# Graph attention and a gated FFN on one core: attention in slots of two units, with steps of the output projection in the last slots

## The chip, the cores and the metric

The kernel runs on one core of a Trainium2 chip. The metric is the device time of one execution in microseconds (us). All times below are in us unless a unit stands beside them. Lower is better.

## The reference

The input `x` has 384 rows (nodes) of 1024. A layer of graph attention with 16 heads of 64 is followed by a gated FFN, both with a residual.

```python
def _L0_gnn_ref(x, edge_index, edge_type, edge_type_weights, wq, bq, ...):
    q = x @ wq.T + bq
    k = x @ wk.T + bk
    v = x @ wv.T + bv
    q2 = (q @ wiq.T + biq).reshape(N, H, D).transpose(1, 0, 2)
    k2 = (k @ wik.T + bik).reshape(N, H, D).transpose(1, 0, 2)
    v2 = (v @ wiv.T + biv).reshape(N, H, D).transpose(1, 0, 2)
    mask = _build_mask(edge_index, edge_type, edge_type_weights, x.dtype)
    scores = jnp.einsum('hnd,hmd->hnm', q2, k2) * scale + mask[None]
    attn = jax.nn.softmax(scores, axis=-1)
    out = jnp.einsum('hnm,hmd->hnd', attn, v2)
    out = out.transpose(1, 0, 2).reshape(N, OUT_F)
    return out @ wo.T + bo

def _L0_ffn_ref(x, w1_w, w1_s, w2_w, w2_s, h1_w, h1_s, h2_w, h2_s, w3_w, w3_s):
    h = jax.nn.silu(_tlin(x, w1_w, w1_s)) * _tlin(x, w2_w, w2_s)
    h = jax.nn.gelu(_tlin(h, h1_w, h1_s), approximate=False)
    h = jax.nn.gelu(_tlin(h, h2_w, h2_s), approximate=False)
    return _tlin(h, w3_w, w3_s)

x = x + _L0_gnn_ref(_layernorm(x, axis=-1), edge_index, ...)
x = x + _L0_ffn_ref(_layernorm(x, axis=-1)[None], ...)[0]
```

The mask is built from 12288 edges: minus infinity where there is no edge, and a positive weight by the type of the edge where there is one.

## The kernel before

All matrices of attention are float32. The kernel works through these stages, and TensorE (PE) goes through them in this order:

- The layer norm of `x` and its transposition into `xT`, behind 34 transposes of the identity that nobody reads (`warm`, L222).
- Four projections with `matmul_T` (L138): q, q2, v and later k. Each output chunk of 128 columns is a sum of 8 matmuls of 384 columns in one bank of the PSUM pool `ps_mm`, and ScalarE (ACT) moves it out with its bias. v2 is made with `matmul_R` (L147), whose matmuls have 512 columns. Meanwhile GpSimd (POOL) scatters the 12288 edges into a table in DRAM, from which the mask `nmask` is read back.
- Attention. A *unit* `u` is one tile of 128 query rows for one pair of heads: 8 pairs times 3 row tiles make 24 units. `scores(u)` is two matmuls of 64 rows, one per head. `exponentials(u)` is, per head, one reduce on VectorE (DVE), which adds the mask, writes `s` and finds the row's minimum `lo` (the scores are negated), and one exp on ACT, which writes `e` and the row's sum. `normalised(u)` is a reciprocal and two multiplications of `e` on DVE. `transposed(u)` is 6 transposes on PE into two banks `pp`; ACT copies the first to `pT`, DVE the second. When the three units of a pair are done, `weighted(pair)` makes `av` in 6 matmuls, two heads side by side in the array's columns, and ACT copies it to `aT`.
- k2, the projection of k, is not made ahead as a whole. `project_k2` (L421) is a generator of 64 steps, one matmul each. Chunks 0 to 2 (24 steps) come first, and the remaining 40 steps are spread over the loop of units.
- The output projection with `wo`: 6 groups of 8 matmuls of 512 columns, one for each row tile `t` and half (`project_out`, L536). Behind each group DVE adds the residual (L539) and takes statistics (L113), and behind each second group comes the layer norm of the tile.
- The FFN (`rest`, L581). It has two forms. The fast one multiplies in a rounded type, with the activations split into two rounded parts. It is exact if the weights of the FFN have no low mantissa bits. To know that, the kernel reads all FFN weights as integers in 16 pieces (`inspect`, L176): per piece one DMA `raw` and two operations on DVE that OR the bits together into `bits` (L182). `gather_bits` (L548) reduces `bits` to one word per partition, the matmul `fl` (L575) adds the words over the partitions, and the result is the flag of the branch (L566, L684). 6 of the 16 pieces are read during the projection of k. The other 10 are read around wo: 5 ahead of it, 3 after its first group, and 2 after the first row tile's layer norm.

The kernel writes the order of SP, ACT, DVE and PE out by hand: each engine works in the order in which the program names its instructions (`manual_schedule`, L58). The order inside the loop of attention before the change is, for each unit `u`:

```python
scs = scores(u) if u < units else None
pt = transposed(u - 2) if 2 <= u < units + 2 else None
if pt:
    nc.scalar.copy(*pt[0])
if 1 <= u <= units:
    normalised(u - 1)
if scs:
    exponentials(u, scs)
if pt:
    nc.vector.tensor_copy(*pt[1])
if u >= 3 and (u - 3) % NT == NT - 1:
    weighted((u - 3) // NT)
```

Then comes the unit's share of k2, two steps in most units. The last steps of k2 are done in unit 19. [...]

## Time and profile before

| What | Value |
|---|---|
| Runs | 426.0, 426.37, 426.67 (median 426.37) |
| Profiled execution, its own time | 426.34 |
| Its span, first to last instruction | 424.6 |
| PE busy | 408.7 (96%) |
| DVE, ACT, POOL busy | 177.4, 100.0, 109.5 |
| Matmuls of k2 (L426) | 128 records, 45.5 busy |
| Matmuls of scores (L442), av (L484) | 96 records each |
| Matmuls of wo (L152) | 96 records, 41.8 busy |
| Mean granted clock of TensorE | 0.994 |

A float32 matmul appears as two records of the profile, so 128 records of k2 are 64 matmuls; a transpose is one record. Matmuls are pipelined, so the busy time of a record overlaps that of the next, and the time between two starts says more than a record's length. The chain of waits is followed back from the last instruction: at each step to what released it, or to the instruction ahead of it on its engine. Its times and the times of the timeline count from the start of the span.

### The profile page before, as it was taken

The page shows a single profiled execution, that of the slowest core. Times are in us where ns is not written, and L with a number is a line of the kernel's source. Part 1 is how long each engine was busy: PE and PEld are TensorE (multiplying, and loading weights), DVE is VectorE, ACT ScalarE, POOL GpSimd, SP SyncE. Part 2 cuts the span into 40 slices and gives each one's busy share as a digit, 9 for nine tenths or more (in the row PEclk, how much of TensorE's full clock was granted, in tenths as well). Part 3 has the DMA queues.
Part 4 walks back from the last instruction along what each step waited for, and adds up shares of the span by engine and source line. Part 5 has one row for each costly group of instructions (what it writes and reads, how often), then busy time and mean ns, then how long its engine had stood idle before and what let it go on. Part 6 is the DMA issues. An engine that isn't in the chain of part 4 may idle for free.

```text
span 424.6 us, 4305 instructions
## 1 busy us (share of the span) xinstructions
PE 408.7 (96%) x1549; PEld 242.4 (57%) x1549; DVE 177.4 (42%) x563; ACT 100.0 (24%) x220; POOL 109.5 (26%) x117
## 2 busy tenths in 40 slices
PE   7899999999999999999999999999999999999991
PEld 6555555555555444455555454455544445799971
DVE  5646879300000010124000476666678755232462
ACT  4511111111111000011111565455462002222510
POOL 3023335234747475734473000000000000200000
PEclk9999999999999999999999999999999999999997
DMA  7699855986050505085425060000196100920012
GB/s 266 215 357 260 267 164 189 393 313 199 0 199 0 199 6 192 19 319 177 180 55 200 2 175 25 0 0 2 34 377 243 42 0 2 298 99 0 2 72 80
DMA packets 29207, 59.64 MB, mean 140 GB/s; under 512 B 4384, under 2 KB 7296, under 8 KB 29056
## 3 DMA queue, kind: packets, MB, share of 16 engines
q1 hardware_dynamic: 22016, 49.89, 34.0%
q0 software_dynamic: 6880, 9.03, 7.4%
q10 hardware_dynamic: 288, 0.41, 0.3%
q8 instruction: 14, 0.23, 0.2%
q14 instruction: 9, 0.07, 0.0%
HBM read 57.06 MB, written 2.26 MB: 140 GB/s over the span
## 4 chain that ended last, share of the span: by engine, by line
PE 90%; DMA 3%; DVE 3%; ACT 2%; issue 0%; SPq 0%; ACTq 0%; DVEq 0%
PE ps L143 39%; PE ps L152 19%; PE ps L426 9%; PE ps L590 6%; PE sc L442 5%; PE pp L475 4%; PE av L484 4%; PE ps L603 3%; DMA out<-y 2%; DMA xs<-in_x 1%; PE pt L531 1%; ACT e L459 1%; DVE y L680 1%; DVE y L681 1%; DVE st L113 0%
## 5 line engine op out<-in xcount | busy, mean ns | idle before, releaser
L353 POOL DMA_INDIRECT tab<-val,cell x96 | 94.1, 980 | 119.2 <-DMA tab<-val,cell 65.1
L426 PE MATMUL ps<-kT,wik 128*128 128x384 f32 x128 | 45.5, 492 | 0.0
L337 DVE SCALAR_TENSOR_TENSOR jk<-kr,key,later 128x256 bf16<-128x256 f32 x96 | 40.0, 479 | 13.0 <-DMA kr<-keyd 12.6
L402 DVE TENSOR_TENSOR v<-ps,row 128x512 f32<-128x512 f32 x6 | 4.2, 692 | 96.1 <-PE ps L152 96.1
L456 DVE CUSTOM_DVE_ANT_0 s<-sc,nmask 128x384 f32<-128x384 f32 x48 | 24.7, 552 | 43.5 <-PE sc L442 43.5
L152 PE MATMUL ps<-wo,aT 128*128 128x512 f32 x96 | 41.8, 593 | 0.0
L143 PE MATMUL ps<-xT,wq 128*128 128x384 f32 x128 | 41.5, 487 | 0.3 <-ACT xT L257 0.3
L143 PE MATMUL ps<-qT,wiq 128*128 128x384 f32 x128 | 41.4, 486 | 0.0
L143 PE MATMUL ps<-xT,wv 128*128 128x384 f32 x128 | 41.4, 486 | 0.0
L143 PE MATMUL ps<-xT,wk 128*128 128x384 f32 x128 | 41.4, 486 | 0.0
L152 PE MATMUL ps<-wiv,vT 128*128 128x512 f32 x96 | 41.4, 592 | 0.0
L143 PEld LDWEIGHTS ps<-xT,wk 128*128 128x128 f32 x128 | 24.3, 190 | 17.2 <-issue 0.5
L143 PEld LDWEIGHTS ps<-xT,wq 128*128 128x128 f32 x128 | 24.2, 190 | 17.2 <-ACT xT L257 0.5
L143 PEld LDWEIGHTS ps<-qT,wiq 128*128 128x128 f32 x128 | 24.3, 190 | 17.0
L143 PEld LDWEIGHTS ps<-xT,wv 128*128 128x128 f32 x128 | 24.3, 190 | 17.0
L426 PEld LDWEIGHTS ps<-kT,wik 128*128 128x128 f32 x128 | 22.7, 190 | 15.7 <-issue 4.1
L152 PEld LDWEIGHTS ps<-wiv,vT 128*128 128x128 f32 x96 | 18.2, 190 | 22.7 <-issue 22.5
L152 PEld LDWEIGHTS ps<-wo,aT 128*128 128x128 f32 x96 | 18.0, 190 | 22.1 <-issue 21.3
L459 ACT ACTIVATE e<-s,lo 128x384 f32<-128x384 f32 x48 | 29.1, 608 | 4.6 <-DVE lo L456 4.5
L182 DVE TENSOR_TENSOR bits<-bits,raw 128x512 int32<-128x512 int32 x32 | 22.1, 691 | 15.7 <-DMA raw<-in_w 14.8
L590 PE MATMUL ps<-x,w 128*128 128x384 f32 (+2 forms) x176 | 25.8, 306 | 0.0
L590 PEld LDWEIGHTS ps<-x,w 128*128 128x128 f32 x176 | 25.1, 190 | 0.5 <-issue 0.5
(110 smaller groups left out, 360.7 us busy)
## 6 DMA issues: line engine op xcount, KB each, us to landing
kr<-keyd SPq DMA_DIRECT2D x11, 576.0 KB, 5.8
raw<-in_w SPq DMA_DIRECT2D x12, 512.0 KB, 4.2
w<-in_w POOLq DMA_DIRECT2D x3, 2048.0 KB, 9.3
wiq<-in_wiq SPq DMA_DIRECT2D x2, 2048.0 KB, 12.8
wv<-in_wv SPq DMA_DIRECT2D x2, 2048.0 KB, 15.3
wiv<-in_wiv SPq DMA_DIRECT2D x2, 2048.0 KB, 14.4
wk<-in_wk SPq DMA_DIRECT2D x2, 2048.0 KB, 8.3
wik<-in_wik SPq DMA_DIRECT2D x2, 2048.0 KB, 7.7
```

Source lines behind the costliest of these rows:

```text
L143: nc.tensor.matmul(ps[:, :N], lhsT=w[:, k, o * P:(o + 1) * P], rhs=src[:, k, :], start=(k == 0), stop=(k == nk - 1))
L152: nc.tensor.matmul(ps[:, :w.shape[2]], lhsT=src[:, k, t * P:(t + 1) * P], rhs=w[:, k, :], start=(k == 0), stop=(k == nk - 1))
L182: nc.vector.tensor_tensor(bits, bits, raw[:, h * FH:(h + 1) * FH].bitcast(I32), op=ALU.bitwise_or)
L337: nc.vector.scalar_tensor_tensor(jk[:, :w], krf[:, j * P:j * P + w], key[:, c:c + 1], later[:, :w], op0=ALU.is_equal, op1=ALU.mult, accum_ ...
L353: i = nc.gpsimd.indirect_dma_start(out=tab, in_=val[:, c:c + 1], in_offset=None, out_offset=bass.IndirectOffsetOnAxis(ap=cell[:, c:c + 1], ...
L426: nc.tensor.matmul(ps[:, :N], lhsT=wik[o // 4][:, k, o % 4 * P:(o % 4 + 1) * P], rhs=kT[:, k, :], start=(k == 0), stop=(k == KF - 1))
L442: nc.tensor.matmul(sc[:, :N], lhsT=q2T[r, pair, t * P:(t + 1) * P], rhs=k2T[r, pair, :], start=True, stop=True)
L456: nc.vector.tensor_tensor_reduce(s, sc[:, :N], nmask[:, t, :], 1.0, 3e38, op0=ALU.add, op1=ALU.min, accum_out=lo)
L459: nc.scalar.activation(e, s, AF.Exp, bias=lo, scale=-1.0, accum_out=dens[u][:, j:j + 1])
L475: nc.tensor.transpose(pt[:, m, :], e[:, m * P:(m + 1) * P], ident)
L484: nc.tensor.matmul(av[j * D:(j + 1) * D, :N], lhsT=v2[:, m, h * D:(h + 1) * D], rhs=pTs[pair % 2][:, j * NT + m, :], start=(m == 0), stop= ...
L590: nc.tensor.matmul(ps[:, rows], lhsT=w[:, k, o * P:(o + 1) * P], rhs=x[:, k, rows], start=n == 0, stop=n == len(todo) - 1)
```

## The change

- Attention goes in 13 slots: unit 0, eleven slots of two units, unit 23. A slot is: the scores of its units, the reduces and exps of its units, the av of a pair that is complete since two slots ago, the transposes of the first unit of the slot before, the slot's share of k2, and the transposes of the second one. A unit is normalised in its own slot.
- The share of k2 is 7 steps in slot 0, and 3 or 4 in slots 1 to 10. In slots 11 and 12 three steps each of the first group of wo take its place. After the last slot stand more steps of wo: one and six, then the transposes of unit 23, one and four, the last av, and three. So three groups of wo are at 7 of 8 steps when the loop ends; `project_out` finishes them first.
- Two pieces of the inspection come ahead of the last transposes; the rest stay at their places.
- The exp writes over the buffer that the reduce wrote: one pool `e` of 9 buffers in place of `s` (3) and `e` (6).
- A first exp of one column (`loaded`) stands ahead of k2, and with it the load of the exp table on ACT.
- PSUM: `ps_mm` has 2 banks instead of 3; `ps_ff`, now opened ahead of attention with 4, holds the scores and wo's groups; `ps_pt` has 2. Behind attention the transposes of `x2` have their own 2 banks (`ps_out`), and the FFN's banks go two of `ps_ff`, one of `ps_mm`.

```diff
-    ps_mm = ctx.enter_context(tc.tile_pool(name="ps_mm", bufs=3, space=bass.MemoryType.PSUM))
+    ps_mm = ctx.enter_context(tc.tile_pool(name="ps_mm", bufs=2, space=bass.MemoryType.PSUM))
...
+    wos = [queue.pop(0)[0] for _ in range(2)]
     aT = act.tile([P, KF, N], FP, tag="xT", name="aT")
+    ps_ff = ctx.enter_context(tc.tile_pool(name="ps_ff", bufs=4, space=bass.MemoryType.PSUM))
+
+    def bank(name="ps"):
+        return ps_ff.tile([P, 512], FP, tag="ff", name=name)
+
+    def out_steps(ps, t, half, k0, k1):
+
+        for k in range(k0, k1):
+            nc.tensor.matmul(ps, lhsT=aT[:, k, t * P:(t + 1) * P], rhs=wos[half][:, k, :],
+                             start=k == 0, stop=k == KF - 1)
+        return k1
...
-                s = ap.tile([P, N], FP, tag="s", name="s", bufs=3)
+                e = ap.tile([P, N], FP, tag="e", name="e", bufs=9)
                 lo = small.tile([P, 1], FP, name="lo")
-                nc.vector.tensor_tensor_reduce(s, sc[:, :N], nmask[:, t, :], 1.0, 3e38,
+                nc.vector.tensor_tensor_reduce(e, sc[:, :N], nmask[:, t, :], 1.0, 3e38,
                                                op0=ALU.add, op1=ALU.min, accum_out=lo)
-                e = ap.tile([P, N], FP, tag="e", name="e", bufs=6)
-                nc.scalar.activation(e, s, AF.Exp, bias=lo, scale=-1.0,
+                nc.scalar.activation(e, e, AF.Exp, bias=lo, scale=-1.0,
                                      accum_out=dens[u][:, j:j + 1])
...
         units = H // 2 * NT
+        slots = [[0], *([u, u + 1] for u in range(1, units - 1, 2)), [units - 1]]
+        loaded = small.tile([P, 1], FP, name="loaded")
+        nc.scalar.activation(loaded, eps, AF.Exp)
         k2 = project_k2()
-        done, rest_k2 = 0, (KF - AHEAD) * KF
+        done, pairs, left = 0, 0, (KF - AHEAD) * KF
         for _ in range(AHEAD * KF):
             next(k2)
-        for u in range(units + 3):
...
+        begun = []
+        for s, new in enumerate(slots):
+            old = slots[s - 1] if s else []
+            scs = [scores(u) for u in new]
+            for u, sc in zip(new, scs):
+                exponentials(u, sc)
+            if s >= 2 and max(slots[s - 2]) >= NT * pairs + NT - 1:
+                weighted(pairs)
+                pairs += 1
+            for i in range(2):
+                if i < len(old):
+                    pt = transposed(old[i])
+                    nc.scalar.copy(*pt[0])
+                    nc.vector.tensor_copy(*pt[1])
+                if i < len(new):
+                    normalised(new[i])
+                if i == 0:
+                    share = min(7 + -(-(left - 7) * s // (len(slots) - 3)), left) - done
+                    for _ in range(share):
+                        next(k2)
+                    done += share
+                    if s >= len(slots) - 2:
+                        if not begun:
+                            begun.append((bank(), 0))
+                        ps, k = begun.pop()
+                        begun.append((ps, out_steps(ps, 0, 0, k, k + 3)))
+        inspect_more(False, 2)
+        out_steps(begun[0][0], 0, 0, KF - 2, KF - 1)
+        begun = [(begun[0][0], KF - 1), (bank(), KF - 1)]
+        out_steps(begun[1][0], 0, 1, 0, KF - 2)
+        pt = transposed(units - 1)
+        nc.scalar.copy(*pt[0])
+        nc.vector.tensor_copy(*pt[1])
+        out_steps(begun[1][0], 0, 1, KF - 2, KF - 1)
+        begun.append((bank(), 4))
+        out_steps(begun[2][0], 1, 0, 0, 4)
+        weighted(pairs)
+        out_steps(begun[2][0], 1, 0, 4, KF - 1)
+        begun[2] = (begun[2][0], KF - 1)
...
-    ps_ff = ctx.enter_context(tc.tile_pool(name="ps_ff", bufs=5, space=bass.MemoryType.PSUM))
+    ps_out = ctx.enter_context(tc.tile_pool(name="ps_out", bufs=2, space=bass.MemoryType.PSUM))
...
     def project_out(t, half, st):
         c = slice(half * FH, (half + 1) * FH)
-        ps = matmul_R(wos[half], aT, t)
+        ps, k = begun.pop(0) if begun else (bank(), 0)
+        out_steps(ps, t, half, k, KF)
         nc.vector.tensor_add(xs[:, t, c], ps, xs[:, t, c])
         statistics(t, st, half)
...
-    inspect_more(True, 2)
+    inspect_more(True)
     for t in range(NT):
         st = small.tile([P, 2, 6], FP, name="st")
         project_out(t, 0, st)
...
         def bank():
+            taken.append(len(taken) % 3)
+            if taken[-1] == 2:
+                return ps_mm.tile([P, 512], FP, tag="mm", name="ps")
             return ps_ff.tile([P, 512], FP, tag="ff", name="ps")
```

The loop over the row tiles behind `inspect_more(True)` is as before. For `t` = 0 it is: first half of `project_out`, three pieces of the inspection, second half, layer norm, the last two pieces, `gather_bits`. For `t` = 1: both halves, layer norm, `fl`, the flag, the transposes of the first tile. For `t` = 2: first half, the load of the flag, the transposes of the second tile, second half, layer norm.

## The prediction

> **What bounds the kernel now.** I read the shares of the span first, then the chain of waits, then the timeline of the stretch that is changed.

> ```profile
> PE 408.7 (96%) x1549; PEld 242.4 (57%) x1549; DVE 177.4 (42%) x563; ACT 100.0 (24%) x220; POOL 109.5 (26%) x117
> PE 90%; DMA 3%; DVE 3%; ACT 2%; issue 0%; SPq 0%; ACTq 0%; DVEq 0%
> ```

> TensorE is busy for 96% of the span and is 90% of the chain, so only two things help: less time for the same matmuls, or fewer waits of PE. The chain inside attention, in order of time (start, length, what), shows the period:

> ```profile
> 250.06 0.84 PE sc L442 x4
> 250.90 0.81 PE pp L475 x6
> 251.71 2.09 PE av L484 x12
> 253.79 1.49 PE ps L426 x4
> 255.28 0.85 PE sc L442 x4
> 256.13 0.80 PE pp L475 x6
> 256.93 1.29 PE ps L426 x4
> ```

> A step of k2 or of scores is two records. Two steps of k2 take 1.29, so one takes 0.645. The scores of a unit are two heads on two halves of the array's rows: their streams overlap, yet the group takes 0.845, 0.20 more than one stream. The share of k2 that follows an av takes 1.49, again 0.20 more. The timeline shows PE's waits (in brackets, with what ended them):

> ```profile
> 240.68 1.39 PE L442 MATMUL sc<-k2T,q2T 64*128 64x384 f32 x4 [0.96 <-DVE lo L456]
> 313.89 1.39 PE L442 MATMUL sc<-k2T,q2T 64*128 64x384 f32 x4 [0.86 <-DVE lo L456]
> ```

> Attention on the chain runs from 235.06 (first scores) to 322.57 (first step of wo): 87.5. Its regular pieces are 24 x 0.845 scores, 24 x 0.805 transposes, 40 x 0.645 for k2, 8 x 2.09 for av and 6 x 0.20 after av: 20.3 + 19.3 + 25.8 + 16.7 + 1.2 = 83.3. So 4.2 are waits, nearly all at the two ends, where k2 has not yet spread or has run out.

> Behind attention I read VectorE, because wo and the inspection of the weights' bits share that stretch:

> ```profile
> 320.28 7.22 DVE L182 TENSOR_TENSOR bits<-bits,raw 128x512 int32<-128x512 int32 x10
> 329.74 0.69 DVE L539 TENSOR_TENSOR xs<-ps,xs 128x512 f32<-128x512 f32 x1 [2.24 <-PE ps L152]
> 331.07 4.30 DVE L182 TENSOR_TENSOR bits<-bits,raw 128x512 int32<-128x512 int32 x6
> 336.53 0.69 DVE L539 TENSOR_TENSOR xs<-ps,xs 128x512 f32<-128x512 f32 x1 [1.16 <-PE ps L152]
> 339.29 2.86 DVE L182 TENSOR_TENSOR bits<-bits,raw 128x512 int32<-128x512 int32 x4
> 342.18 2.23 DVE L553 TENSOR_TENSOR bits<-bits 128x256 int32<-128x256 int32 x9
> 344.71 0.69 DVE L539 TENSOR_TENSOR xs<-ps,xs 128x512 f32<-128x512 f32 x1
> 350.16 0.19 PE L575 MATMUL fl<-ones,bitf 128*1 128x1 f32 x2
> ```

> The matmul `fl` needs `bitf`, which VectorE finishes just before 344.71. PE comes to `fl` at 350.16, 5.4 later. That is the slack the change spends.

> **The change, part by part.** All against the profiled execution: 426.34, of which 424.6 is span; the median of the runs is 426.37, 0.03 off.

> *Slots of two units.* The two scores groups stand back to back, so I take 2 x 0.645 + 0.20 = 1.49 for four heads instead of 1.69: 11 slots save 2.2. Two groups in a row do not occur in the trace. The bounds are nothing saved (each group pays its 0.20) and 2.2; I take 2.2, because the 0.20 appears where the kind of matmul changes, not inside a run of one kind. An av now comes after scores and before transposes; the 0.20 of k2 after an av goes (1.2). Transposes after an av stand in the trace at 318.10 and show no such surplus: their first copy starts 0.58 after them, as elsewhere. Av straight after scores is unseen: bounds 0 and 7 x 0.20 = 1.4 lost; I take 0, since av after transposes shows none.

> *Waits inside attention.* I laid the new order of PE, VectorE and ScalarE out by these durations: a reduce each 0.48, an exp each 0.61, a copy 0.48, a normalisation 0.87. Unit 0's softmax took 5.1 (235.06 to 240.16), of which 1.28 was the table load that is moved ahead; the 3.8 left lie under seven steps of k2 (4.5), so the wait at 240.68 goes. The wo steps cover the last slots and the last transposes. What is late next is slot 10, with three steps of k2 and no av. The last transposes of the slot could start at 1.49 + 0.8 + 1.94 + 0.4 = 4.6 after its start. The copy that frees their bank stands behind four exps on ScalarE: first reduce 1.55 after the start (VectorE still normalises the slot before), 0.65 to the first exp, 4 x 0.61, copy 0.48: 5.1. So 0.5, and with 0.2 elsewhere 0.7. The same laying-out gives 3.6 of the 4.2 that the kernel before shows, so I book 1.2. PSUM costs nothing: a projection's bank has 5.2 until its next use and the eviction takes 0.58; were that cover gone, each of 40 chunks would cost 0.6.

> *wo moved forward.* 18 of the 48 steps of 0.858 (two records of 0.429) now lie before the last av. They are the same work: 15.4. The end of the last av becomes 235.06 + 2 x 0.845 + 11 x 1.49 + 19.3 + 25.8 + 16.7 + 15.4 + 1.2 = 331.6. Before, the comparable point is 322.57 + 15.4 = 338.0. The gain up to here is 6.4.

> *The price behind it.* Wo's first three groups are finished almost together, so from the last av PE has only 3 + 3 + 8 = 14 steps, 12.0, before it reaches `fl`. VectorE's queue in front of `bitf` is: two pieces of bits early and three more under the last wo steps (hidden), then the first add, which needs 4 steps and a latency of 0.3 (3.75 after the av); add and statistics, 1.33 (329.74 to 331.07); six bit operations, 4.30; second add, statistics, moments and normalisation, 2.76 (336.53 to 339.29); four bit operations, the tree and the casts, 5.42 (339.29 to 344.71). The sum is 17.6. PE waits 17.6 - 12.0 = 5.6 at `fl`, with everything queued behind it: the transposes of x2, the last 16 steps of wo, the flag, the FFN. The loads of raw are not late: the last trio needs the first pT buffer free, over 20 before VectorE reads it. Net 6.4 - 5.6 = 0.8 gained, 425.5, if nothing else happens.

> *The clock.* An idle PE of 5.6 occurs nowhere inside the kernel before. Only its two ends show what idleness does. The table by stretches (length, PE busy, PEld, DVE, ACT, POOL, then granted clock):

> ```profile
> 418.00:419.00 1.00, 0.00 (x0) 0.00 (x0) 0.00 (x0) 0.00 (x0) 0.00 (x0) 1.00 0.32 111
> 419.00:420.00 1.00, 0.00 (x0) 0.00 (x0) 0.00 (x0) 0.00 (x0) 0.00 (x0) 0.75 0.10 30
> 420.00:421.00 1.00, 0.00 (x0) 0.00 (x0) 0.43 (x1) 0.00 (x0) 0.00 (x0) 0.50 0.02 7
> ```

> The last matmul ends at 415.25; the granted clock is halved from about 419.5, 4.25 later. At the other end, the loads of the warming transposes (min/median/max ns, first and last start):

> ```profile
> L225 PEld LDWEIGHTS pw<-ident x6: 231/231/231, 4.3 to 5.4; 128*128 128x128 f32 x6
> L225 PEld LDWEIGHTS pw<-ident x10: 139/140/142, 8.2 to 9.2; 128*128 128x128 f32 x10
> ```

> They begin at 2.33 and turn from 231 to 140 ns at about 6.4, after 4.0 of work; the clock column reads 1.00 there, so only durations show it. 5.6 exceeds 4.25, so I expect half the clock when `fl` starts, for about 4.0, which loses half of that: 2.0. Bounds: 0 (the clock holds) and 4.0 (twice as long a slow stretch). I take 2.0.

> [...]

> *The FFN.* Same matmuls, six banks in turn and two for transposes instead of five; its waits on the chain (1.7 at 397, 1.7 at 403) are on gelu, not on banks: 0.

> Sum: 426.34 - 6.4 + 5.6 + 2.0 = 427.5.

> **The rivals.**
> 1. *The clock holds.* [...] For it: 5.6 is only 1.3 over the one drop that the trace shows. Against: the drop is there. Time 425.5, on the faster side.
> 2. *Attention gains less.* Each scores group pays its 0.20 (2.2) and av after scores too (1.4): 427.5 + 3.6 = 431.1. For it: 0.845 against 0.645 in every unit. Against: no surplus where transposes meet av.
> 3. *VectorE is not late at `fl`* (the queue is shorter than I read): no wait, no clock: 426.34 - 6.4 = 419.9. Against: every operation of it is in the rows above, in that order.

> **How the numbers follow.** A measurement of this kernel can tell about 0.2% (0.85) from no change. The forecast (wait and clock) has 0.61, with its own range 426.3 to 429.5; rival 1 has 0.24, between 424.5 and 426.5; rival 2 has 0.09; rival 3 has 0.02; 0.04 is left for more gain in attention, near 424. Slower: about three quarters of the forecast (0.46), all of rival 2: 0.55. Within 0.2%: 0.15 of the forecast, 0.11 of rival 1: 0.26. Faster: the rest, 0.19. For the range I take 425.0 to 430.0: it holds the forecast, most of rival 1, and leaves out rivals 2 and 3.

> **What would show it.** Right: scores x8 of about 1.5 in one slot; no wait of PE near 240; an idle PE of 5 to 6 ended by `bitf` in front of `fl`; a clock of 0.5 in the stretch behind it, and steps of wo of twice 0.858 there. Wrong: `fl` without a wait, a clock of 1.00 throughout, or waits of PE on VectorE in every slot.

## The result, and the profile after

The changed kernel takes 425.25 us (median of 12 runs, 423.69 to 427.02) against 426.37; the ratio is 0.9975 with a 95% interval of 0.9958 to 0.9991. The median is lower by a quarter of a per cent. The forecast was 427.5, on the other side. The median stands in a gap: six of the 12 runs lie between 423.69 and 424.79, six between 425.70 and 427.02; the experiments e6 and e8 come back to these two levels.

The profiled execution took 424.21, of which the span is 422.4. The shares of the span and of the chain of waits:

```profile
PE 404.6 (96%) x1549; PEld 245.0 (58%) x1549; DVE 176.0 (42%) x563; ACT 98.1 (23%) x221; POOL 110.9 (26%) x117
PE 90%; DVE 5%; ACT 2%; DMA 2%; issue 1%; SPq 0%; ACTq 0%; DVEq 0%
```

VectorE, 3% of the chain before, is now 5%. The chain inside attention (start, length, what), a slot without an av and one with:

```profile
257.48 1.49 PE sc L460 x8
258.97 0.80 PE pp L492 x6
259.77 2.58 PE ps L444 x8
262.36 0.65 PE pp L492 x6
263.01 1.49 PE sc L460 x8
264.50 2.09 PE av L501 x12
266.59 0.80 PE pp L492 x6
267.39 1.94 PE ps L444 x6
```

The scores of two units take 1.49, as forecast, and av straight behind scores still takes 2.09. The transposes are 0.80 behind scores or av, but only 0.65 behind k2. The timeline of PE shows a single wait above 0.5 inside attention, and then the one behind it:

```profile
301.85 0.55 PE L492 MATMUL pp<-ident,e 128*128 128x128 f32 x3 [0.67 <-ACT pTb L530]
329.96 12.28 PE L423 MATMUL ps<-wo,aT 128*128 128x512 f32 x28
347.64 0.19 PE L611 MATMUL fl<-ones,bitf 128*1 128x1 f32 x2 [5.39 <-DVE bitf L592]
347.76 1.97 PE L572 MATMUL pt<-ident,xn 128*128 128x128 f32 x8
349.52 8.38 PE L423 MATMUL ps<-wo,aT 128*128 128x512 f32 x16
```

The wait at 240.68 is gone, the one in slot 10 is there (0.67), and `fl` waits 5.39 for `bitf`. VectorE works through it:

```profile
342.08 2.86 DVE L182 TENSOR_TENSOR bits<-bits,raw 128x512 int32<-128x512 int32 x4
...
347.43 0.15 DVE L592 CAST bitf<-bits 128x1 f32<-128x1 int32 x1
```

The table by stretches (length, PE, PEld, DVE, ACT and POOL busy, granted clock) shows the clock halved during the wait and for a while behind it:

```profile
345.00:346.00 1.00, 0.00 (x0) 0.00 (x0) 0.92 (x3) 0.00 (x0) 0.00 (x0) 0.70 0.00 0
346.00:347.00 1.00, 0.00 (x0) 0.00 (x0) 0.84 (x5) 0.00 (x0) 0.00 (x0) 0.50 0.00 0
352.00:353.00 1.00, 1.00 (x3) 0.45 (x2) 0.38 (x1) 1.00 (x3) 0.00 (x0) 0.89 0.00 0
```

Up to the FFN the two profiles differ by little: its first matmul starts at 365.42 before and at 365.07 after. The other 1.9 of the spans' 2.2 lies at the end, 1.7 of it in one write of the output, whose lines the change does not touch. This is the last write on the chain of the kernel before:

```profile
416.41 4.05 DMA out<-y
```

And this is the one on the chain of the changed kernel:

```profile
415.96 2.39 DMA out<-y
```

### The profile page after: what moved, and what is told of

It reads as the page before. It is cut to its first block, busy times and chain, and to the rows that moved or that the text cites. A ratio compares the mean times of both kernels' runs of the same rounds, so it can differ in the third digit from the quotient of the medians.

```text
span 422.4 us, 4320 instructions
## 1 busy us (share of the span) xinstructions
PE 404.6 (96%) x1549; PEld 245.0 (58%) x1549; DVE 176.0 (42%) x563; ACT 98.1 (23%) x221; POOL 110.9 (26%) x117
## 4 chain that ended last, share of the span: by engine, by line
PE 90%; DVE 5%; ACT 2%; DMA 2%; issue 1%; SPq 0%; ACTq 0%; DVEq 0%
PE ps L143 39%; PE ps L152 10%; PE ps L444 9%; PE ps L423 8%; PE ps L626 6%; PE ps L639 5%; PE av L501 4%; PE pp L492 4%; PE sc L460 4%; DVE bits L182 2%; DMA xs<-in_x 1%; PE pt L572 1%; DVE st L113 1%; ACT e L476 1%; DMA out<-y 1%
## 5 line engine op out<-in xcount | busy, mean ns | idle before, releaser
L353 POOL DMA_INDIRECT tab<-val,cell x96 | 95.4, 993 | 118.1 <-DMA tab<-val,cell 67.5
L423 PE MATMUL ps<-wo,aT 128*128 128x512 f32 x96 | 43.8, 609 | 0.0
L444 PE MATMUL ps<-kT,wik 128*128 128x384 f32 x128 | 43.5, 488 | 0.0
L152 PE MATMUL ps<-wiv,vT 128*128 128x512 f32 x96 | 41.4, 592 | 0.0
L474 DVE CUSTOM_DVE_ANT_0 e<-sc,nmask 128x384 f32<-128x384 f32 x48 | 23.9, 553 | 37.8 <-PE sc L460 37.8
L476 ACT ACTIVATE e<-e,lo 128x384 f32<-128x384 f32 x48 | 29.0, 604 | 25.1 <-DVE lo L474 25.1
L152 PEld LDWEIGHTS ps<-wiv,vT 128*128 128x128 f32 x96 | 18.2, 190 | 22.7 <-issue 22.5
L182 DVE TENSOR_TENSOR bits<-bits,raw 128x512 int32<-128x512 int32 x32 | 22.1, 691 | 14.4 <-DMA raw<-in_w 13.6
L626 PE MATMUL ps<-x,w 128*128 128x384 f32 (+2 forms) x176 | 25.8, 307 | 0.0
```

The lines of the kernel that those rows point to most:

```text
L152: nc.tensor.matmul(ps[:, :w.shape[2]], lhsT=src[:, k, t * P:(t + 1) * P], rhs=w[:, k, :], start=(k == 0), stop=(k == nk - 1))
L182: nc.vector.tensor_tensor(bits, bits, raw[:, h * FH:(h + 1) * FH].bitcast(I32), op=ALU.bitwise_or)
L353: i = nc.gpsimd.indirect_dma_start(out=tab, in_=val[:, c:c + 1], in_offset=None, out_offset=bass.IndirectOffsetOnAxis(ap=cell[:, c:c + 1], ...
L423: nc.tensor.matmul(ps, lhsT=aT[:, k, t * P:(t + 1) * P], rhs=wos[half][:, k, :], start=k == 0, stop=k == KF - 1)
L444: nc.tensor.matmul(ps[:, :N], lhsT=wik[o // 4][:, k, o % 4 * P:(o % 4 + 1) * P], rhs=kT[:, k, :], start=(k == 0), stop=(k == KF - 1))
L474: nc.vector.tensor_tensor_reduce(e, sc[:, :N], nmask[:, t, :], 1.0, 3e38, op0=ALU.add, op1=ALU.min, accum_out=lo)
```

## The experiments

Ten kernels ran. Each expectation names a theory and a rival, and what each of them would show. Ratios are against the kernel before, measured beside them, with 95% intervals.

**The flag late (e1).** The last two pieces and the tree stand behind the second tile's layer norm, and `make_flag` (the lines of `fl` and the flag's copy) in the middle of wo's last group:

```diff
         elif t == 2:
-            low_bits = nc.values_load(flag[0:1, 0:1], min_val=0, max_val=P * 0xFFF)
             transpose_x2(1)
+            ps = bank()
+            out_steps(ps, t, 1, 0, 4)
+            flag = make_flag()
+            out_steps(ps, t, 1, 4, 7)
+            low_bits = nc.values_load(flag[0:1, 0:1], min_val=0, max_val=P * 0xFFF)
+            begun.append((ps, 7))
         project_out(t, 1, st)
         layernorm(t, xn[:, t, :], st)
-        if t == 0:
-            inspect_more(False, len(pieces))
-            bitf = gather_bits()
-        elif t == 1:
...
+        if t == 1:
+            transpose_x2(0)
+            inspect_more(False, len(pieces))
+            bitf = gather_bits()
```

> The changed kernel with the tail of the inspection reordered: the last two pieces and the reduction of the bits come behind the second tile's layer norm on VectorE, and the matmul fl stands in the middle of the last group of wo. Nothing is left out. Theory (what attention saved goes to PE's wait at fl and to the slow clock behind it): fl waits for nothing, the granted clock stays 1.00 from 330 to 400, and the time falls by the wait of 5.4 and the 2.3 that the slow stretch cost (transposes of x2 1.90 instead of 0.87, 16 records of wo 8.17 instead of 6.87): 425.3 - 7.7 = 417.6. Rival (VectorE bounds this stretch, so the wait only moves to the transposes of x2 or to the flag): 423 or more, with a PE wait of 3 or more somewhere between 340 and 370.

Measured: 418.45, ratio 0.9816 (0.9791 to 0.984). PE's timeline and one row of the table by stretches:

```profile
342.15 1.06 PE L572 MATMUL pt<-ident,xn 128*128 128x128 f32 x8
...
354.32 0.19 PE L597 MATMUL fl<-ones,bitf 128*1 128x1 f32 x2
```

```profile
345.00:350.00 5.00, 5.00 (x13) 2.12 (x12) 3.69 (x8) 1.99 (x4) 0.00 (x0) 1.00 0.01 3
```

No bracket stands at `fl`, the clock is 1.00, and the FFN starts at 357.58, 7.5 earlier than in the changed kernel. The theory stands: attention's saving was there, and the wait and the clock took it.

**PE kept busy in front of `fl` (e2).**

```diff
+            pw = ps_out.tile([P, 4, P], FP, tag="out", name="pw")
+            for i in range(40):
+                nc.tensor.transpose(pw[:, i % 4, :], ident, ident)
             fl = ps_mm.tile([P, 512], FP, tag="mm", name="fl")
```

> The changed kernel with 40 transposes of the identity, which nobody reads, on PE in front of fl. bitf is ready at the same moment, so PE comes no further by them; only its idleness falls from 5.4 to about 1. Theory (the slow clock behind the wait costs 2.3 by itself): clock 1.00 in the stretch behind fl, transposes of x2 0.87, 16 records of wo 6.87, and 425.3 - 2.3 = 423.0. Rival (the stretch behind fl is slow for another reason, such as VectorE and ScalarE reading and writing beside it): those lengths stay, 425.3.

Measured: 423.66, ratio 0.9926 (0.9901 to 0.9951). Timeline of PE:

```profile
342.06 4.53 PE L612 MATMUL pw<-ident 128*128 128x128 f32 x40
347.63 0.19 PE L614 MATMUL fl<-ones,bitf 128*1 128x1 f32 x2 [1.03 <-DVE bitf L592]
347.75 1.09 PE L572 MATMUL pt<-ident,xn 128*128 128x128 f32 x8
348.68 7.03 PE L423 MATMUL ps<-wo,aT 128*128 128x512 f32 x16
```

The clock in its table by stretches:

```profile
345.00:350.00 5.00, 3.97 (x29) 2.98 (x28) 4.59 (x15) 0.00 (x0) 0.00 (x0) 1.00 0.00 0
```

`fl` starts at the same 347.63. Behind it, start to start, the transposes take 0.93 instead of 1.76 and the 16 records of wo 6.86 instead of 8.21: 2.18, and the FFN starts 2.18 earlier (362.89). Forty useless transposes hold the clock at 1.00 and save 2.2 in the profile, so the halved clock has a price of its own. Between the medians it is 1.6. For e1 and e3, too, the medians differ from the changed kernel's by 0.7 and 0.8 less than the FFN's start does (6.8 and 3.7 against 7.5 and 4.5); that fits what the changed kernel's six runs on the lower level take off its median (425.25, against 425.87 for the other six).

**The slots without early wo (e3).**

```diff
-                    if s >= len(slots) - 2:
...
-                        begun.append((ps, out_steps(ps, 0, 0, k, k + 3)))
-        inspect_more(False, 2)
-        out_steps(begun[0][0], 0, 0, KF - 2, KF - 1)
-        begun = [(begun[0][0], KF - 1), (bank(), KF - 1)]
-        out_steps(begun[1][0], 0, 1, 0, KF - 2)
         pt = transposed(units - 1)
         nc.scalar.copy(*pt[0])
         nc.vector.tensor_copy(*pt[1])
-        out_steps(begun[1][0], 0, 1, KF - 2, KF - 1)
-        begun.append((bank(), 4))
-        out_steps(begun[2][0], 1, 0, 0, 4)
         weighted(pairs)
-        out_steps(begun[2][0], 1, 0, 4, KF - 1)
-        begun[2] = (begun[2][0], KF - 1)
+        inspect_more(False, 2)
```

> The slots, the early table load and the exp in place stay, but no step of wo stands in front of the last av: all 48 follow it, and the two early pieces of the inspection stand behind it. Theory: PE has waits of 2 to 3 in the last slots and at the last av, which now ends near 317.3, but behind it stand 28 more records, so VectorE has bitf before PE asks; no wait at fl, clock 1.00. FFN from about 360.4 instead of 365.1: 425.3 - 4.7 = 420.6. Rival (the wo steps in the last slots are what attention gained, and the price behind them is small): at or above 425.

Measured: 421.53, ratio 0.9881 (0.9856 to 0.9905). Timeline of PE:

```profile
307.76 0.87 PE L492 MATMUL pp<-ident,e 128*128 128x128 f32 x6 [0.93 <-ACT pTa L530]
...
312.76 0.88 PE L492 MATMUL pp<-ident,e 128*128 128x128 f32 x6 [0.38 <-ACT pTb L530]
313.88 1.02 PE L492 MATMUL pp<-ident,e 128*128 128x128 f32 x6 [0.24 <-DVE e L484]
...
317.63 27.73 PE L423 MATMUL ps<-wo,aT 128*128 128x512 f32 x64
345.29 0.19 PE L596 MATMUL fl<-ones,bitf 128*1 128x1 f32 x2
```

The uncovered waits are back: the last av ends at 317.63, where the changed kernel's 330.03 less its 15.4 of early wo would make 314.6, so early wo had covered 3.0. The brackets are 1.55 of that, and the last av takes 2.65 in the timeline, where the changed kernel's takes 2.16; the rest is not split further. Yet the FFN starts at 360.55, 4.5 earlier than in the changed kernel, because 64 records of wo stand between the last av and `fl` instead of 28 (36 more, not 28 as the expectation has it), and `fl` waits for nothing.

**The table load alone (e4),** in the kernel before:

```diff
+        loaded = small.tile([P, 1], FP, name="loaded")
+        nc.scalar.activation(loaded, eps, AF.Exp)
         k2 = project_k2()
```

> The kernel before with one edit: the one-column exp ahead of k2, which moves the load of the exp table to an idle ScalarE. Theory: the load of 1.28 stood on the chain between the first reduce and the first exp and goes from PE's wait near 240.7 (0.96, and 0.54 inside that scores group): 426.4 - 1.3 = 425.1, as much as the whole change brought. Rival: the wait near 240.7 is set by VectorE's order (unit 0 is normalised in front of unit 1's reduces), and the load is only part of it: 0 to 0.5 gained.

Measured: 425.08, ratio 0.997 (0.9951 to 0.9988). The scores that waited 0.96 and started at 240.68 now start without a wait:

```profile
239.65 1.14 PE L442 MATMUL sc<-k2T,q2T 64*128 64x384 f32 x4
```

The median is 1.3 lower, so one instruction brought as much as the whole change.

**The output in places of its own (e6 in the changed kernel, e8 in the kernel before).**

```diff
+        if fast:
+            ys, yat = act.tile([P, NT * F], FP, tag="xT", name="ys"), 0
...
-                y = stage.tile([P, FH], FP, tag="stage", name="y")
                 n = b - a
+                if fast:
+                    y, yat = ys[:, yat:yat + n], yat + n
+                else:
+                    y = stage.tile([P, FH], FP, tag="stage", name="y")
```

> The changed kernel, with the seven pieces of the output each in a place of its own (in the buffer of aT, dead by then) instead of two buffers in turn. Nothing else differs. In the profiles the last piece waits for the third-last write to land, 4.0 to 4.3 in five kernels and 2.4 in the profile of the change alone. Theory (the end of every kernel is set by these two buffers, and how long the writes take there differs from run to run; it is no effect of the change): the last y is done about 3.2 after the last full piece begins, the end falls by 3.3 against a run with the long write, and the runs lie closer together: 422.5. Rival (the write to the output is bound by itself, not by the buffers): 425, same spread.

> The kernel before with the same edit of the output's places. With the tail taken out of both, the difference between this one and the changed kernel with that edit is what the change does up to the FFN. Theory (8.0 saved in attention, 5.4 waited at fl, 2.3 lost to the slow clock; the rest of the profiles' difference of 2.1 was the write at the end): 426.4 - 3.3 = 423.1, and the changed one lies 0.3 to 0.6 below it. Rival (the other banks of the FFN or an earlier PE made the end shorter by 1.9): the changed one lies 2 below it.

Measured: 421.88 (ratio 0.9933, 0.9908 to 0.9959) and 422.83 (0.994, 0.9918 to 0.9962). In both, no write stands on the chain between the pieces any more: the fifth piece waits for PE (until 412.40 and 413.40), and the last two follow it without a wait. The runs of the kernel before lie on two levels, 424.4 to 424.8 and 425.9 to 427.0: 1 of the first 12 was on the lower one, 5 of the next 17, 9 of the 17 after these, 4 of the last 12. The profiles fit them: before and e1 to e4 were profiled in a run on the upper level of their kernel and show a last write of 3.95 to 4.31, the changed kernel in one on the lower level, with 2.39. With the edit the six runs of the kernel before lie between 422.4 and 423.2, on one level. So the two levels are put down to the two buffers and the writes that free them, and the theory of the tail holds for the kernel before. In the changed kernel the edit leaves a spread of 1.9: four runs from 421.6 to 421.9, two from 423.2 to 423.5. The kernel e7 below has the same edit and no halved clock, and its five runs lie within 0.5; that points to the clock, without showing it run by run, and the clock's cost differed by only 0.9 between the profiles.

Without the tail the change is worth 421.88 - 422.83 = -0.95, a difference of medians of six runs each, with that spread. The profiles agree: FFN from 364.43 in e6 and from 365.46 in e8, 1.0 apart. That lies between the theory's 0.3 to 0.6 and the rival's 2; the extra is the clock, which cost 1.7 in e6's profile (transposes 1.76, wo 7.71) where it cost 2.2 in the first. From the FFN's start to the fifth piece of the output it is 48.0 in both (to 412.43 and 413.43), so the FFN's other banks cost nothing.

**Both mends (e7, the edits of e1 and e6 together), and in e7 one step of k2 moved from slot 0 to slot 10 (e11).**

> Both mends together: the flag late, and the output in places of its own. Theory: 418.4 - 3.3 = 415.1, clock 1.00 up to the end of the last matmul, no PE wait above 0.7 between 240 and 390. Rival: the mends overlap (the write at the end sets the time anyway), 417.

> The kernel with both mends, and one step of k2 moved from slot 0 to slot 10 (shares 6, 4, 3, 3, 4, 3, 3, 4, 3, 3, 4). Theory (slot 10 has no av, and three steps do not cover the four exps ahead of the copy that frees the bank): the PE wait of 0.67 in the second half of slot 10's transposes goes, nothing comes in its place, and the FFN begins 0.5 to 0.7 earlier: about 414.7. Rival (slot 0 needs its seven steps): a wait of the same size appears near 240, 415.3.

```diff
-                    share = min(7 + -(-(left - 7) * s // (len(slots) - 3)), left) - done
+                    share = min(sum([6, 4, 3, 3, 4, 3, 3, 4, 3, 3, 4][:s + 1]), left) - done
```

Measured: 415.31 (ratio 0.9765, 0.9741 to 0.9789) and 414.62 (0.9741, 0.972 to 0.9763). The transposes of slot 10 in e7's timeline, then in e11's:

```profile
301.82 0.55 PE L492 MATMUL pp<-ident,e 128*128 128x128 f32 x3 [0.67 <-ACT pTb L530]
```

```profile
300.70 1.06 PE L492 MATMUL pp<-ident,e 128*128 128x128 f32 x6
```

The wait is gone, none came near 240, and the FFN starts at 357.10 instead of 357.70. Both mends add up to what was expected, and e11 is the fastest kernel of the study, 2.6% below the one before.

**Av apart (e9) and scores apart (e10),** both with the output's own places, against e6. In e9 the av stands behind the first transposes of the slot:

```diff
-            if s >= 2 and max(slots[s - 2]) >= NT * pairs + NT - 1:
-                weighted(pairs)
-                pairs += 1
...
                 if i == 0:
+                    if s >= 2 and max(slots[s - 2]) >= NT * pairs + NT - 1:
+                        weighted(pairs)
+                        pairs += 1
```

In e10 the second unit's scores do:

```diff
-            scs = [scores(u) for u in new]
-            for u, sc in zip(new, scs):
-                exponentials(u, sc)
+            exponentials(new[0], scores(new[0]))
...
                 if i == 0:
+                    if len(new) == 2:
+                        exponentials(new[1], scores(new[1]))
```

> The changed kernel with the output's own places, and with one order changed in the slots: av stands behind the first transposes of a slot, in front of k2's share, as before the change, instead of straight behind the scores. Theory (whatever follows a group on a part of the array pays 0.15 to 0.20, transposes and k2 alike, and an av straight behind scores shares that one payment): seven slots with an av pay once more, 7 x 0.17 = 1.2 above the kernel with the output's places alone; the chain shows k2's share longer by 0.20 behind each av, and transposes of 0.81 behind scores. Rival (av costs the same wherever it stands): no difference.

> The changed kernel with the output's own places, where the scores of a slot's second unit stand behind the first transposes, in front of k2's share, instead of beside the first unit's. Theory (two groups of scores together save the 0.20 of the second one, and the exit of 0.15 to 0.20 that whatever follows pays): groups of 0.85 twice instead of 1.49 once, and k2's share longer by 0.20, in 11 slots: 11 x 0.40 = 4.4, plus waits of about 2 where the later reduces now delay copies and chunks: last av near 334.5 to 336 instead of 329.9, time 427 to 428. Rival (the pairing itself is worth nothing, the shape of the slots is): the chain shows no longer groups and the last av stays within 2 of 329.9.

Measured: 424.16 (0.9966, 0.9949 to 0.9983) and 427.75 (1.0052, 1.0033 to 1.0072). The chain of e9:

```profile
252.89 2.09 PE av L501 x12
254.97 2.13 PE ps L444 x6
257.11 0.66 PE pp L492 x6
```

and of e10:

```profile
255.29 0.85 PE sc L460 x4
256.14 2.13 PE ps L444 x6
258.27 0.65 PE pp L492 x6
```

Three steps of k2 take 2.13 behind an av or scores and 1.94 behind transposes. In e9 the last av ends 1.76 later than in e6 (331.59 against 329.83), of which 7 x 0.19 = 1.3 is this surplus; 0.2 already stood at the first scores (235.21 against 235.00 on the chains), and the other 0.2 stays open. Of the 2.3 between the two medians, the 0.5 beyond that is in the profiles the clock again: transposes of x2 and 16 records of wo behind `fl` took 1.76 and 8.21 in e9's profile, 0.5 more than in e6's. In e10 the last av ends at 335.29, 5.5 later: 11 x 0.21 from two groups of 0.85 for one of 1.49, 10 x 0.19 from k2's shares, and new waits, the longest 1.7. Both theories stand, on what the chains show.

## Why the prediction was wrong

Five of its steps were right, most within 0.3. Two groups of scores cost 1.49; av behind scores cost nothing more (2.09), and k2 behind transposes lost its 0.20; the wait of slot 10 stood where it was put (0.5 foreseen, 0.67 measured); `fl` waited 5.39 where 5.6 was foreseen; and the clock fell to a half and took 2.2 where 2.0 was booked. Rivals 2 and 3 fell with the groups of 1.49 and the wait of 5.39, and rival 1 with the clock of 0.50. Rival 1's 425.5 is near the measured time by luck: the clock that it left out cost 2.2, and attention's larger gain and the end of the kernel made up for it.

The waits and the clock were right; the step that failed is a term of the sum that was mis-sized: the transposes in "The end of the last av becomes ...": 19.3 for 24 x 0.805. In the kernel before every group of transposes but the last two stands behind scores, so its groups inside attention showed only 0.805. In the change one of each two stands behind k2 or wo, where it takes 0.65 to 0.71. Of the 24 groups 12 moved there: 12 x 0.145 = 1.7. The last av ended at 330.03, not 331.6, and attention gained 8.0 instead of 6.4. The runs show a surplus on transposes and on k2 alike: the transposes took 0.80 behind scores or av and 0.65 behind k2 in the changed kernel, and three steps of k2 took 2.13 behind av in e9 and behind scores in e10, where they took 1.94 behind transposes in the changed kernel. The prediction saw that surplus twice, behind av (0.20 on k2) and inside scores, but not in the 0.805 itself. Its argument from the transposes behind an av, at 318.10, sets them against transposes behind scores, which pay the same. The rows for it were in the trace before. This is the chain's row of the 8 transposes of x2, behind wo:

```profile
358.24 0.87 PE pt L531 x8
```

They take 0.109 each, where the 6 behind scores take 0.134 each. And these are two rows of PE's timeline, a share of k2 straight behind the scores of the first unit, and what follows it:

```profile
235.84 1.56 PE L426 MATMUL ps<-kT,wik 128*128 128x384 f32 x4
237.32 0.92 PE L442 MATMUL sc<-k2T,q2T 64*128 64x384 f32 x4
```

From start to start it takes 1.48, 0.19 more than the 1.29 behind transposes; the share behind the second unit's scores has the same length (1.56). The prediction's split of attention leaves these two out, and counts six shares of k2 behind an av where the chain has five, so its waits of 4.2 are about 0.2 too large.

With the measured 8.0, 5.4 and 2.2 the sum is -8.0 + 5.4 + 2.2 = -0.4, so 425.9, inside the range and within 0.2% of no change. The rest, from 425.9 to 425.25, is put down to the write at the end, which differs by 1.7 between the two profiles. The execution that the sum starts from is on the upper level, and the changed kernel's six runs there have a median of 425.87. Over the runs, 6 of its 12 lie below 425 against 1 of the 12 beside them, while later the kernel before had 9 of 17 on its lower level. So this part of the median is the draw of the runs, as far as these counts tell; why the write takes 2.4 in some runs and 4.0 in others was not settled. Compared without those buffers, the change gains 0.95.

The forecast of slower rested on a difference of large terms: 6.4 gained against 7.6 lost. An error of 1.6 in one of them turned the sign. That 425.25 still lies in the range, near its lower end, is luck: that end was there for a clock that holds, and the clock did not hold. The range of the unseen costs was drawn for scores and av alone, and the transposes, whose neighbour changed too, were taken at one price.

## What to carry to other kernels

When work is moved forward out of a stretch, ask what it was covering there: 18 steps of wo filled 3 or so of waits and uncovered a queue on VectorE that cost 5.4, and 2.2 more through the clock. When an order changes, price each piece by its new neighbour, not by its mean in the old order. Before a schedule is rebuilt, look for single instructions on the chain: one table load moved, or seven output places instead of two buffers, each brought as much as the whole change or more.

## What the runs showed of the hardware

```profile
344.00:345.00 1.00, 0.00 (x0) 0.00 (x0) 0.93 (x3) 0.00 (x0) 0.00 (x0) 0.62 0.00 0
351.00:352.00 1.00, 1.00 (x4) 0.44 (x3) 0.58 (x3) 0.83 (x2) 0.00 (x0) 0.97 0.00 0
```

It began 2.1 (e6), 3.2 (changed kernel), 3.1 (e9) and 4.0 (e10) after PE's last matmul, so the same idleness cost 1.7, 2.2, 2.2 and 2.6. The longest waits of PE between its first and its last matmul are 0.96 in the kernel before and 5.39 in the changed kernel; in e10 one of 1.71 stands ahead of the 5.38. No run shows what a wait between 1.7 and 5.4 does to the clock.
